# Layer 0's transfers taken off ScalarE: v written by GpSimd, blocks and rows loaded by SyncE

## The chip, the cores and the metric

The kernel runs on one core of one Trainium2 chip. A core has a matrix engine (TensorE, PE in the profile; its weight loads are shown as PEld), a vector engine (VectorE, DVE), an engine for activations and copies (ScalarE, ACT), a general engine (GpSimd, POOL) and a sequencer that only issues transfers and waits (SyncE, SP). Transfers can be issued by SyncE, ScalarE and GpSimd, each with a queue of its own (q1, q10 and q0 in the profile); all queues are served by the same 16 DMA engines. Each engine works through its own list of instructions in order and waits where an instruction needs something that another engine or a transfer has not delivered. The metric is the time of one execution on the device in microseconds (us).

## What is computed

An input x of 8 images of 56 x 56 pixels with 384 channels goes through two layers in float32, each of the form x + conv(groupnorm(x)). The "conv" of a layer is an attention over 3 x 3 neighbourhoods:

```python
# layer 0: 12 heads, a 9 x 9 attention per pixel and head
v = einsum('bhwc,oc->bhwo', x, Wv)
patches = the 3 x 3 neighbours of each pixel of v, zero outside the image
a = einsum('bhwc,oc->bhwo', x, Wa).reshape(b, n, heads, 9, 9)
attn = softmax(a * d ** -0.5, axis=-1)
out = einsum('bnhpq,bnqhd->bnphd', attn, patches)
# each of the 9 rows p of out is added back to the neighbour that it belongs to, then
y = einsum('bhwc,oc->bhwo', canvas, Wo)
# layer 1: 6 heads, one row of 9 weights per pixel and head, biases, no adding back
```

The group norm has 32 groups over whole images, so its statistics must be complete before a layer's values of that image are used.

## The kernel before

Images are taken two at a time: four pairs. Within a pair the work goes by image columns: 56 columns of 2 x 56 = 112 pixels, which lie on the partitions. Eight columns make a group, and since 7 tiles of 128 rows hold the 8 x 112 pixels, the eighth column's pixels ride along in the last 16 rows of the seven tiles; at the eighth step no tile is computed.

Layer 0 is one loop over 4 x 56 steps and three more. A step is `attend` for one column, with pieces of other work put between its matmuls by `between`:

- TensorE projects the column's normalised input `xn` on the attention weights `wa_t` in three parts into PSUM banks (three banks, used in turn). VectorE takes the maximum and subtracts it into `at`, ScalarE applies the exponential, then TensorE makes the values in another bank and ScalarE copies them to `v`, which has two buffers.
- `spread` writes v to a table in DRAM, `vtab0`, laid out by patches of 7 columns with 2 columns of margin on each side. A column that two patches need is written twice by one transfer. The last 16 rows are written to the place of the group's eighth column, by one or two further transfers. In the kernel before these two or three transfers are issued by ScalarE right behind the copy of v.
- One step later `weigh` runs `normalise` (VectorE sums to `den`, GpSimd multiplies `at` by it) and, for the column before, `presum` (GpSimd adds neighbouring columns into `pre`). `share_out` sends the 16 rows of `at` to their place by GpSimd transfers (`last`, `at<-at`, `at<-last`).
- Three steps later `fold` turns `pre` into rows of weights `wts`: GpSimd clears a buffer, ScalarE fills two rows, TensorE shifts (`pw`), VectorE adds the rest, and SyncE writes it to a second table, `ztab0`. There are four `wts` buffers.
- Once in seven steps `fetch_v` loads a patch's values (`vp`, two transfers of 1536 KB) and, a step later, `fetch` its weights (`z`, two of 2352 KB) on SyncE. From four steps after that, `contract` multiplies them on TensorE into two PSUM tiles `pc`, which ScalarE copies to `yT`; `project_out` multiplies by the output weights into `po`, VectorE adds the residual `xres` into `x1t`, and SyncE stores it. These pieces are queued in `jobs`, two a step.

The input is made ready beside this. The pair's transposed input lies in DRAM (`xTs`). `load` brings a block of four columns into `xin`, of which there is one buffer, at the step where `j == NCH - 1`, that is once in four steps, behind the last `normed` that reads the block before; `normed` makes `xn` of it two steps later on ScalarE. For the next pair `stats_load` brings four columns of rows into `xr` (two buffers), once in three steps; TensorE transposes them (`pt`), ScalarE copies them to `xt`, VectorE takes statistics and SyncE writes them to `xTs`. In the kernel before, `load` and `stats_load` are issued by ScalarE, from `upkeep`, at the end of a step.

Two things set the order. In layer 0's loop every engine keeps the order of the program: `tc.keep_in_program_order` and the class `InOrder` (lines 124 to 134) record it. Transfers report through counters: those of SyncE and ScalarE share one set of eight, used in turn, those of GpSimd have another eight. A transfer is not issued until the one that used its counter before has landed.

Layer 1 is a second loop after this one. It is not touched; its own `spread` is already issued by GpSimd.

Of the kernel before, what the change touches and what calls it, by code (L numbers as in the profile page):

```python
# [15 lines left out]
def two_outlook_layers(  # L16
# [34 lines left out]
    B, H, W, C = x.shape  # L51
# [7 lines left out]
    SB = 8  # L59
# [266 lines left out]
    def spread(queue, table, width, col, pad, row, v, rows_of=None):  # L326

        (px, sx), *more = patches_of(col, pad)
        n, rows = 1 + len(more), v.shape[0]
        line = width * C  # L330
        first = (px * (R + GAP) + GAP + row) * line + sx * C
        queue.dma_start(  # L332
            bass.AP(
                table.tensor, table.offset + first,
                [
                    *([line * step, count] for step, count in rows_of or ((1, rows),)),
                    *([[(R + GAP) * line - PX * C, n]] if n > 1 else []), [1, C],
                ],
            ),
            v.unsqueeze(1).to_broadcast([rows, n, C]) if n > 1 else v,  # L340
        )
# [79 lines left out]
    def layer0(late, pools):  # L421
# [11 lines left out]
        def stats_load(pair, blk, queue, xr):  # L433
            queue.dma_start(xr, xf[pair * R : (pair + 1) * R, blk * XB : (blk + 1) * XB, :])
            xrs[pair, blk] = xr

        def xr_tile(pair, blk):
            return io.tile([P, XB, C], F32, tag="xr", name=f"xr_{pair}_{blk}")[:R]
# [121 lines left out]
        def load(g):  # L560
            pair, blk = divmod(g, NBLK)
            xins[g] = io.tile([P, NCH, XB, R], F32, tag="xin", name=f"xin_{g}", bufs=1)
            scalar.dma_start(
                xins[g].rearrange("p i m r -> p i (m r)"),
                xTs[pair][:, :, blk * XB * R : (blk + 1) * XB * R],
            )
# [24 lines left out]
        def attend(pair, c, between):  # L591

            nm = f"0_{pair}_{c}"
            k, j = divmod(c, SB)
            if j == NTILE:
                for n in range(K + 1):
                    between(n)
                return
            lhs = xns[(pair * W // SB + k) % 2][:, :, j, :]
            at = work.tile([P, K, K2, PH], F32, tag="at", name=f"at_{nm}", bufs=4)  # L600
            mx = work.tile([P, K, PH], F32, tag="mx", name=f"mx_{nm}", bufs=1)
            for pi in range(K):
                pl = bank(P, BANK - NP0, BANK)
                project(pl[:, :NL], lhs, wa_t, pi * NL, NL)
                pl = pl.rearrange("r (q a) -> r q a", q=K2)
                vector.tensor_reduce(mx[:, pi, :], pl.rearrange("r q a -> r a q"), AX.X, ALU.max)
                vector.tensor_tensor(
                    at[:, pi], pl, mx[:, pi, :].unsqueeze(1).to_broadcast([P, K2, PH]), ALU.subtract
                )
                between(pi)  # L610
            scalar.activation(at, at, AF.Exp, scale=SCALE0)
            attns[pair, c] = at
            pv = bank(P, 0, C)
            project(pv, lhs, wv_t, 0, C)
            v = work.tile([P, C], F32, tag="v", name=f"v_{nm}")
            scalar.copy(v, pv)
            spread(scalar, vtab0, SX0, c, 2, 0, v[:R])
            end = c - j + NTILE
            if len([*patches_of(end, 2)]) == 1:
                spread(scalar, vtab0, SX0, end, 2, j * PART, v[R:], ((H, IMG), (1, PART)))  # L620
            else:
                for b in range(IMG):
                    lo = R + b * PART
                    spread(scalar, vtab0, SX0, end, 2, b * H + j * PART, v[lo : lo + PART])
            between(K)

        def share_out(pair, c):

            k, j = divmod(c, SB)
            at, last = attns[pair, c], lasts[(pair * W // SB + k) % 2]  # L630
            if j < NTILE - 2:
                gpsimd.dma_start(
                    bass.AP(
                        last.tensor, last.offset + j * PART * NA0,
                        [[H * NA0, IMG], [NA0, PART], [1, NA0]],
                    ),
                    at[R:].rearrange("p a b c -> p (a b c)"),
                )
                return
            end = c - j + NTILE  # L640
            if j == NTILE - 2:
                attns[pair, end] = work.tile([P, K, K2, PH], F32, tag="at", name=f"at_0_{pair}_{end}", bufs=4)
                for b in range(IMG):
                    n = b * H + j * PART
                    gpsimd.dma_start(
                        attns[pair, end][b * H : n].rearrange("p a b c -> p (a b c)"), last[b * H : n]
                    )
            for b in range(IMG):
                n, lo = b * H + j * PART, R + b * PART
                gpsimd.dma_start(attns[pair, end][n : n + PART], at[lo : lo + PART])  # L650
# [184 lines left out]
        def upkeep(step):  # L835

            pair, c = divmod(step, W)
            if pair == 0:

                for n in (2 * step, 2 * step + 1):  # L840
                    if n < NBLK:
                        keep_block(0, (0, 1, 4, 2, 3)[n] if n < 5 else n)
                if c == 1:
                    gpsimd.memset(wts, 0.0)
                if c == 3:
                    sync.dma_start(wo_t, wo0.rearrange("(i p) n -> p i n", p=P))
                if c == 8:
                    for z in zs:
                        nc.gpsimd.memset(z, 0.0)
            while clearing and clearing[0][0] <= step:  # L850
                clearing.pop(0)[1]()
            if pair + 1 < NPAIR:
                blk, i = divmod(c - 3, NCH)
                if 0 <= c and i == 0 and blk < NBLK - 1:
                    stats_load(pair + 1, blk + 1, scalar, xr_tile(pair + 1, blk + 1))
                if NBLK * NCH + 3 <= c < NBLK * NCH + 6:
                    if c == NBLK * NCH + 3:
                        making["0"] = norm_params(stats.pop(pair + 1), f"0_{pair + 1}", params, pair + 1)
                    next(making["0"])
            g, j = divmod(step + 2 * XB, XB)  # L860
            if j < NCH and g < NPAIR * NBLK:
                normed(g, (j,))
            if step < NCH:
                normed(1, (step,), shared=False)
            if j == NCH - 1 and 2 < g + 1 < NPAIR * NBLK and g > 2:
                load(g + 1)
# [14 lines left out]
        for step in range(NPAIR * W + LAG):  # L881
            folding = fold(*divmod(step - LAG, W)) if step >= LAG else iter(())
            turning = turned(step)

            def weigh():

                normal = 1 <= step < NPAIR * W + 1 and (step - 1) % SB < NTILE
                if normal:
                    normalise(*divmod(step - 1, W))
                if normal and step % SB == NTILE:  # L890
                    share_out(*divmod(step - 1, W))
                if 2 <= step < NPAIR * W + 2:
                    presum(*divmod(step - 2, W))
                if normal and step % SB < NTILE:
                    share_out(*divmod(step - 1, W))

            def between(n):

                if n == 0:
                    next(turning, None)  # L900
                    weigh()
                    jobs.run(step, 1)
                elif n == 1:
                    next(folding, None)
                    next(turning, None)
                elif n == 2:
                    jobs.run(step, 1)
                else:
                    next(folding, None)
                    if step % SB == NTILE:  # L910
                        jobs.run(step, 1)

            if step < NPAIR * W:
                attend(*divmod(step, W), between)
                upkeep(step)
            else:
                for n in range(K + 1):
                    between(n)
            flush()

            pair, c = divmod(step - LAG - PX, W)
            if pair >= 0 and c % PX == 0:
                fetch_v(pair, c // PX)
            pair, c = divmod(step - LAG - PX - 1, W)
            if pair >= 0 and c % PX == 0:
                fetch(pair, c // PX, step + 4)
# [336 lines left out]
```

## Time and profile before

| | us |
|---|---|
| three runs | 3550.32, 3551.01, 3561.62 |
| median | 3551.01 |
| profiled execution | 3572.52 |
| its span, from first to last instruction | 3570.8 |
| busy in the span: PE, DVE, POOL, ACT | 3252.5, 1861.3, 1409.7, 1303.7 |
| idle of PE between 71 and 2345 us (layer 0's loop) | 235.6 |
| mean granted PE clock in that stretch, share of full | 0.95 |

The profile is of one execution, whose own time is 21.5 us above the median. A row of instructions gives the line, the engine, the operation, what is written and what is read, how often, the busy time, the mean time of one in ns, and the idle time of the engine just before it with what ended it. Since all work goes through recording helpers, most instructions have line 119, 122 or 134, and are told apart by the names of what they write and read. A row of waits names who waited, for whom, the total, how often and the longest. [...] PE's granted clock is either 1.0 or 0.5 in the records of this run; a mean in between is a mixture over time.

### The profile page before, as it was taken

Reading aid. Unit: us, or ns where it says so; the run is one execution under the profiler, and the core shown is the slowest. Engines: PE = TensorE matmul, PEld = TensorE weight load, DVE = VectorE, ACT = ScalarE, POOL = GpSimd, SP = SyncE. Lnnn points to the kernel's source line nnn. Section 1 sums busy time; section 2 is a strip of 40 time slices with the busy share of each in tenths; the row PEclk is TensorE's granted clock in tenths of the full one; section 3 lists DMA queues with packets and bytes.
Section 4 is the critical chain, followed back from the end, with each engine's and each line's share of the span. In section 5 each row is a group of like instructions: output and inputs, shape, how many; then the busy total and the mean of one; then the engine's idle time right before and its main releaser. Section 6 shows DMA issues by size and latency. Waiting matters only on the chain.

```text
span 3570.8 us, 74251 instructions
## 1 busy us (share of the span) xinstructions
PE 3252.5 (91%) x28510; PEld 2222.9 (62%) x28510; DVE 1861.3 (52%) x4454; ACT 1303.7 (37%) x3315; POOL 1409.7 (39%) x2468
## 2 busy tenths in 40 slices
PE   7777889999898999998998999978999999999998
PEld 5555666666666666666765666645666666666665
DVE  5555665666676666666666577623223323333332
ACT  4333334333333333333433333322434343434432
POOL 2543454444455544455545555531212222222220
PEclk7889999999999999999999999988999999999998
DMA  6788897787788876888786678786787787878785
GB/s 194 227 279 257 271 292 247 247 278 261 247 258 270 268 241 224 272 280 278 223 261 229 218 258 270 234 282 181 215 218 222 220 224 217 230 217 230 213 226 146
DMA packets 618370, 859.13 MB, mean 241 GB/s; under 512 B 207255, under 2 KB 508503, under 8 KB 613919
## 3 DMA queue, kind: packets, MB, share of 16 engines
q1 hardware_dynamic: 445310, 600.76, 54.6%
q10 hardware_dynamic: 127968, 145.91, 13.8%
q0 software_dynamic: 44736, 107.72, 9.6%
q8 instruction: 224, 3.67, 0.4%
q14 instruction: 132, 1.07, 0.1%
HBM read 520.28 MB, written 330.40 MB: 238 GB/s over the span
## 4 chain that ended last, share of the span: by engine, by line
PE 61%; DMA 21%; DVE 7%; issue 4%; ACT 3%; POOL 2%; ACTq 1%; SPq 1%; DVEq 0%; POOLq 0%
PE bank L119 32%; PE po L119 15%; PE pc L119 8%; DMA z<-ztab 6%; DMA ztab<-wts 4%; DMA at<-lgtab 3%; DMA lgtab<-lgt 3%; PE pw L119 2%; ACT xn L134 2%; DMA x<-x1t 2%; DVE den L134 1%; DVE d L134 1%; PE pt L122 1%; DMA xr<-in_x 1%; DVE mx L134 1%
## 5 line engine op out<-in xcount | busy, mean ns | idle before, releaser
L119 PE MATMUL bank<-wa_t,xn 128*128 128x288 f32 x3528 | 984.1, 417 | 35.4 <-ACT xn L134 27.0
L119 PE MATMUL po<-yT,wo_t 128*128 128x448 f32 (+1 forms) x2304 | 831.6, 501 | 47.5 <-DVE x1t L134 44.9
L119 PEld LDWEIGHTS bank<-wa_t,xn 128*128 128x128 f32 x3528 | 660.9, 195 | 253.2 <-issue 26.4
L134 POOL TENSOR_TENSOR at<-at,den 128x972 f32<-128x972 f32 x196 | 441.2, 2251 | 935.2 <-DVE den L134 613.7
L119 PEld LDWEIGHTS po<-yT,wo_t 128*128 128x128 f32 x2304 | 430.8, 192 | 339.6 <-issue 190.1
L332 POOL DMA_DIRECT2D vtab<-v x392 | 214.0, 549 | 846.1 <-DVE v L134 822.4
L119 PE MATMUL pc<-z,vp 121*32 121x49 f32 (+1 forms) x17664 | 390.0, 225 | 138.4 <-ACT yT L134 116.1
L134 DVE TENSOR_REDUCE mx<-bank 128x36 f32<-128x324 f32 x588 | 285.5, 486 | 438.2 <-PE bank L119 435.3
L134 ACT ACTIVATE at<-at 128x972 f32<-128x972 f32 (+1 forms) x228 | 215.4, 945 | 767.9 <-DVE at L134 767.8
L119 PE MATMUL bank<-wc_t,xn 128*128 128x438 f32 x1176 | 482.5, 547 | 2.2 <-ACT xn L134 2.2
L119 PEld LDWEIGHTS pc<-z,vp 121*32 121x32 f32 (+1 forms) x17664 | 352.2, 126 | 205.9 <-ACT yT L134 131.0
L119 PE MATMUL bank<-wv_t,xn 128*128 128x384 f32 x1176 | 436.8, 509 | 1.4 <-issue 1.4
L685 POOL TENSOR_TENSOR pre<-at,at 112x108 f32<-112x108 f32 (+1 forms) x440 | 244.1, 555 | 220.7 <-DMA at<-at 78.1
L119 PEld LDWEIGHTS bank<-wc_t,xn 128*128 128x128 f32 x1176 | 215.9, 193 | 173.7 <-issue 166.9
L134 ACT ACTIVATE xn<-xin,bias,scale 128x168 f32<-128x168 f32 (+1 forms) x474 | 208.4, 502 | 315.1 <-DMA vtab<-v 173.4
L119 PEld LDWEIGHTS bank<-wv_t,xn 128*128 128x128 f32 x1176 | 228.4, 198 | 144.0 <-issue 26.3
L134 DVE TENSOR_TENSOR at<-bank,mx 128x324 f32<-128x324 f32 x588 | 291.4, 496 | 44.1 <-POOL pre L683 13.8
L134 ACT COPY yT<-pc 128x294 f32<-128x294 f32 (+2 forms) x512 | 196.4, 406 | 232.3 <-PE pc L119 227.6
L134 DVE SCALAR_TENSOR_TENSOR x1t<-po,bo_t,x1t 128x448 f32<-128x448 f32 (+1 forms) x156 | 97.6, 626 | 248.5 <-PE po L119 248.5
L134 DVE TENSOR_TENSOR lgt<-bank,ba_t 128x54 f32<-128x54 f32 x196 | 41.6, 212 | 350.5 <-PE bank L119 350.5
L134 ACT ACTIVATE wts<-pre,inside 112x48 f32<-112x48 f32 (+4 forms) x672 | 180.1, 358 | 79.7 <-POOL pre L683 29.0
L134 ACT COPY ot<-pt 112x384 f32<-112x384 f32 x128 | 61.5, 481 | 380.0 <-PE pt L122 325.0
(112 smaller groups left out, 3123.1 us busy)
## 6 DMA issues: line engine op xcount, KB each, us to landing
z<-ztab SPq DMA_DIRECT2D x64, 2352.0 KB
vp<-vtab SPq DMA_DIRECT2D x64, 1536.0 KB
vp<-vtab SPq DMA_DIRECT2D x64, 945.0 KB
xres<-xT SPq DMA_DIRECT2D x32, 1176.0 KB
ztab<-wts SPq DMA_DIRECT2D x336, 110.2 KB
xin<-xT ACTq DMA_DIRECT2D x52, 672.0 KB
vtab<-v ACTq DMA_DIRECT2D x100, 336.0 KB
z<-ztab SPq DMA_DIRECT2D x128, 258.4 KB
```

Of the source, the lines that this page charges most:

```text
L119: tc.keep_in_program_order(nc.tensor.matmul(*args, **kwargs))
L122: tc.keep_in_program_order(nc.tensor.transpose(*args, **kwargs))
L134: return lambda *args, **kwargs: tc.keep_in_program_order(op(*args, **kwargs))
L332: queue.dma_start(bass.AP(table.tensor, table.offset + first, [*([line * step, count] for step, count in rows_of or ((1, rows),)), *([[(R ...
L685: nc.gpsimd.tensor_tensor(dst, terms[0], terms[1], ALU.add)
```

## The change

In layer 0's loop ScalarE issues no transfer any more. The writes of v move from the end of `attend` to a new function `keep_v`, which the following step calls at the end of `weigh`; GpSimd issues them, behind `normalise`, `presum` and `share_out` of that step. The loads of `xin` and `xr` stay where they are in the program, and SyncE issues them. Sizes, targets and buffers are the same.

```diff
         def load(g):
             pair, blk = divmod(g, NBLK)
             xins[g] = io.tile([P, NCH, XB, R], F32, tag="xin", name=f"xin_{g}", bufs=1)
-            scalar.dma_start(
+            sync.dma_start(
                 xins[g].rearrange("p i m r -> p i (m r)"),
...
             v = work.tile([P, C], F32, tag="v", name=f"v_{nm}")
             scalar.copy(v, pv)
-            spread(scalar, vtab0, SX0, c, 2, 0, v[:R])
+            vs[pair, c] = v
+            between(K)
+
+        def keep_v(pair, c):
+
+            j, v = c % SB, vs.pop((pair, c))
+            spread(gpsimd, vtab0, SX0, c, 2, 0, v[:R])
             end = c - j + NTILE
             if len([*patches_of(end, 2)]) == 1:
-                spread(scalar, vtab0, SX0, end, 2, j * PART, v[R:], ((H, IMG), (1, PART)))
+                spread(gpsimd, vtab0, SX0, end, 2, j * PART, v[R:], ((H, IMG), (1, PART)))
             else:
                 for b in range(IMG):
                     lo = R + b * PART
-                    spread(scalar, vtab0, SX0, end, 2, b * H + j * PART, v[lo : lo + PART])
-            between(K)
+                    spread(gpsimd, vtab0, SX0, end, 2, b * H + j * PART, v[lo : lo + PART])
...
-                    stats_load(pair + 1, blk + 1, scalar, xr_tile(pair + 1, blk + 1))
+                    stats_load(pair + 1, blk + 1, sync, xr_tile(pair + 1, blk + 1))
...
                 if normal and step % SB < NTILE:
                     share_out(*divmod(step - 1, W))
+                if normal:
+                    keep_v(*divmod(step - 1, W))
```

More of the change, by code (lines that the diff above doesn't have):

```diff
@@ L623, in attend @@
                     lo = R + b * PART
-                    spread(scalar, vtab0, SX0, end, 2, b * H + j * PART, v[lo : lo + PART])
-            between(K)
+                    spread(gpsimd, vtab0, SX0, end, 2, b * H + j * PART, v[lo : lo + PART])
+        vs = {}
         def share_out(pair, c):
```

## The prediction

> **What bounds the kernel now.** I read first the busy time in stretches, for layer 0's loop (71 to 2345 us) and for one of its holes:
>
> ```profile
> core 0: us, PE busy (x) PEld busy (x) DVE busy (x) ACT busy (x) POOL busy (x), PEclk, DMA share, GB/s
> 71.00:2345.00 2274.00, 2038.36 (x19092) 1453.87 (x19094) 1458.57 (x3555) 821.71 (x1942) 1136.33 (x1947) 0.95 0.79 255
> ...
> 964.50:979.50 15.00, 7.07 (x136) 5.53 (x125) 6.10 (x14) 4.85 (x14) 6.68 (x12) 0.77 0.78 244
> ```
>
> TensorE is busy 2038.4 of the loop's 2274 us: it is the bound, and 235.6 us of idle time are all that removed waits can give, apart from the clock. Next the waits of PE and ACT in the same stretch (total us, times, longest):
>
> ```profile
> PE pc L119 <- ACT yT L134: 93.2, 20, 10.8
> PE po L119 <- DVE x1t L134: 40.1, 24, 12.3
> PE pt L122 <- ACT xt L134: 29.8, 9, 10.9
> PE pw L119 <- POOL pre L683: 23.6, 10, 7.2
> PE bank L119 <- ACT xn L134: 20.9, 7, 5.5
> ```
>
> ```profile
> ACT xn L134 <- DMA vtab<-v: 173.4, 79, 12.4
> ...
> ACT xn L134 <- DMA ztab<-wts: 42.9, 13, 9.5
> ```
>
> PE waits mostly for copies by ScalarE, and ScalarE waits ahead of xn, the work that stands behind v's writes in its program. The timeline shows one case, first ScalarE, then TensorE:
>
> ```profile
> 963.91 0.46 ACT L134 COPY v<-bank 128x384 f32<-128x384 f32 x1
> 971.79 2.08 ACTq L134 DMA_DIRECT2D vtab<-v  x2
> 973.91 1.59 ACT L134 ACTIVATE xn<-xin,bias,scale 128x168 f32<-128x168 f32 x4 [9.54 <-DMA ztab<-wts]
> 975.41 0.51 ACT L134 COPY xt<-pt 128x448 f32<-128x448 f32 x1
> 975.83 0.70 ACT L134 COPY yT<-pc 128x294 f32<-128x294 f32 x2
> ```
>
> ```profile
> 966.72 1.63 PE L119 MATMUL bank<-wa_t,xn 128*128 128x288 f32 x6
> 976.28 2.19 PE L119 MATMUL pc<-z,vp 121*32 121x49 f32 x96 [7.93 <-ACT yT L134]
> ```
>
> ScalarE has finished v at 964.4 but issues its write only at 971.8. The row names what ended the wait: a write of ztab that SyncE had issued. SyncE's and ScalarE's transfers take turns on eight completion counters, so an issue waits until the transfer that had its counter before has landed. That one stood behind the two loads of z issued at 946.1, and v's write, xn, xt and yT stood behind it. PE lost 7.93 us.
>
> **The change, part by part.**
>
> *ScalarE's issues go.* 476 writes of v, 52 loads of xin and 42 of xr leave ScalarE; its stretches between an ACT instruction's end and the last issue add up to 470 us. Most of it costs nothing, as ScalarE is busy 822 of 2274 us. What counts is PE's idle time. I went through PE's gaps over 0.5 us in this stretch one by one: 27 began while, or within 4 us after, ScalarE had stood over 2.5 us at an issue of v. Crediting each with the smaller of the gap and of the standing above 0.55 us an issue gives 110.7 us (10.9, 10.8, 9.4, 7.9 are the largest). This is the first term: **-111**.
>
> *The clock.* In the hole above the granted clock is 0.77, in the loop 0.95. PE was busy for 170 us of the half-rate pieces, which cost 85 us against full rate. The holes credited are 111 of 235.6 us idle, 47%; so I credit 47% of 85: **-40**.
>
> *xin and xr go to SyncE's queue.* 94 issues at 0.57 us (xin's median on ScalarE) are 53 us on SyncE, which in this stretch waits 541 us for wts alone; they cost nothing as such. The load of xin now waits on SyncE for xn of the same step, and behind it stand the next ztab writes, which wait for VectorE's sums anyway, or in some steps a fetch of vp or z, with 5 us of margin at the matmuls (z of the case above had landed at 957.9, its first use is at 963.4). What counts is landing. On ScalarE's queue xin issued at 951.7 landed at 961.0, while z on SyncE's queue landed at 968.7. Behind z it lands after 968.7 plus 2.7 us of its own. I took for each xin the landing of what SyncE had issued before it, plus 2.7 us, and held it against its first use, less the hole that I remove: seven loads are late by 0.4 to 2.3 us (12.4 us) and four by 1.6 to 5.9 us (17.4 us). All of these 30 us on PE's path, with clock in the same ratio (40/111), cost **+41**; nothing if ScalarE's slack hides them. xr, reckoned the same way, has at least 2.8 us left in each case: 0; past that PE's transposes would stand for it directly.
>
> *v's writes go to GpSimd, a step later.* The prices of issues there:
>
> ```profile
> L332 POOL DMA_DIRECT2D vtab<-v x392 | 214.0, 549 | 846.1 <-DVE v L134 822.4 <-issue 11.7 <-DMA z<-ztab 11.5
> ...
> L134 POOL DMA_DIRECT2D last<-at x140 | 86.5, 618 | 1.2 <-POOL at L134 1.2
> ```
>
> 476 issues at 0.549 us (the same write in layer 1) are 261 us; by the row of last, 294. GpSimd idles 2274 - 1136 = 1138 us, so in most steps they fall into its wait for den (935 us ahead of the products at). They are 1.1 to 1.65 us a step, ahead of the memset of wts, which ScalarE reads some 5 us later (1204.5 and 1209.4). In 19 of 196 steps the wait for den is under 1.5 us; these are the seventh columns of the groups of eight, where the chain goes on over a transfer to PE:
>
> ```profile
> 1226.89 1.01 POOL L134 DMA_DIRECT2D at<-at  x2
> 1227.89 0.33 POOL L134 MEMSET wts<- 112x120 f32 x1
> 1229.64 2.25 POOL L134 TENSOR_TENSOR at<-at,den 128x972 f32<-128x972 f32 x1 [1.42 <-DVE den L134]
> ...
> 1238.66 0.41 POOL L685 TENSOR_TENSOR pre<-at,at 112x108 f32<-112x108 f32 x1 [3.06 <-DMA at<-at]
> ```
>
> The later writes hide in the 3.06 us before 1238.66; the earlier ones delay the product by up to 1.65 us. PE waited for pre 10 times. Low bound 0, if the delays end in PE's queue of other work; high bound 28 groups x 1.65 = 46, and 24 more if at's copies wait behind v's bytes for 3 us in the 8 groups that meet a load of z. I take 10 x 1.5: **+15**, nearest to the ten rows seen.
>
> *The buffer of v.* There are two, so the copy of column c+2 waits until v of c has been read. In the short steps, copies two apart are 15.3 us apart; GpSimd gets to the place of the issue 7.8 to 8.2 us after the copy, plus 1.1, so 6.0 us are left for a write that I put at the 5.2 us median and 8.3 us longest of last's transfers on that queue. A lateness of 2.3 us is less than the 4 us until PE needs that bank again. I take **+5**; the high bound is 60 short steps x 2.3 = 138, and 0 the low one. [...]
>
> *What is late next.* In the hole VectorE itself stood 2.41 us for a ztab write (7 such waits, 15.6 us in the loop); these stay: **+15**, between 0 and the 40 of PE's waits for x1t.
>
> Sum: -111 - 40 + 41 + 15 + 5 + 15 = **-75 us**. Against the profiled execution's 3572.5 (span 3570.8) that is 3497; it stands 21.5 us above the median of the runs shown, 3551.0, so the prediction is **3476**.
>
> **Rivals.**
> 1. *The holes go whole.* Nothing new waits: -151, 3400. For it: xin's lateness is small against GpSimd's and ScalarE's idle time. Against: DMA engines are already 0.92 busy at 940 to 964.5.
> 2. *The loads take the wait over.* One queue drains in order, so each xin, xr and ztab write behind 4.7 MB of z is as late as ScalarE was. If half of the 32 patches, not 11 loads, cost 5.3 us and a third of that in clock, the loss is 16 x 7 = 112 on top of the other 35: 3547, no change. For it: ztab issued at 954.9 to 957.8 landed only at 971.4, v's write issued at 956.9 on the other queue at 964.3. [...]
> 3. *Slower: the copy of v waits for GpSimd's write.* If the writes land not 5 to 7 but over 10 us after issue, behind each other and behind z, then margin and bank cover (6 + 4 us) are both gone, and the 60 short steps bind at GpSimd's pace: at 13 us, 60 x 3 = 180 against the 75 gained: 3656; it decides against the change from an 11.3 us landing on. Against: longest row 8.3 us; for: 168 to 336 KB a write, where last has 60.8.
>
> **How the numbers follow.** A measurement of this kernel tells about 0.3% (11 us) from no change. Chances: forecast (3430 to 3525) 0.50, whole gain 0.15, loads take over (3525 to 3575) 0.15, slower by GpSimd's write (3575 and up) 0.20. Faster is the first two and a third of the third: 0.70; same 0.08; slower 0.22. The range runs from 3405, just above the whole gain, to 3585, a third of the way into the slow case: it leaves out 0.07 and 0.13.
>
> **What would show it.** Right: no wait of ACT xn for vtab; PE's wait of pc for yT under 40 us; the loop's PEclk above 0.96; some 261 us more on POOL. xin's step: ACT xn waits for DMA xin 30 us. Wrong: ACT v waiting for vtab's writes by over 100 us, PE pw for pre well over 40, or PE's idle time as before under other names, xin or xr.

## The result, and the profile after

The changed kernel takes 3529.23 us (median of seven runs, 3520.71 to 3542.84); the kernel before, run beside it, 3557.60 (seven runs, 3550.32 to 3573.44). The ratio is 0.9923, 95% interval 0.9899 to 0.9947: 0.8% shorter, 28 us, where 75 were forecast; the whole interval lies below 1. The profiled execution after is one of 3529.23 us, at its median, while the one before (3572.52) lies 15 us above its median; so the two traces differ by 43 us, of which 28 stand in the medians. What is read from the two traces below holds some 15 us that belong to that one execution.

The page of the changed kernel, first the engines' busy time, then v's writes in the groups of instructions (line, engine, operation, count; busy us, mean ns; idle before):

```profile
PE 3245.5 (92%) x28510; PEld 2213.4 (63%) x28510; DVE 1865.4 (53%) x4454; ACT 1297.7 (37%) x3315; POOL 1680.1 (48%) x2944
...
L134 POOL DMA_DIRECT2D vtab<-v x476 | 285.8, 605 | 16.2 <-DMA vtab<-zeros 7.0
```

The stretch of layer 0's loop, in the columns that the prediction shows for before:

```profile
71.00:2302.50 2231.50, 2034.70 (x19097) 1445.08 (x19099) 1461.66 (x3554) 814.01 (x1942) 1406.75 (x2423) 0.95 0.80 259
```

The loop is 42.5 us shorter: 38.8 of it is PE's idle time (235.6 to 196.8), 3.7 its busy time. The granted clock is 0.95 as before. Layer 1 is where it was (1225.8 and 1225.0 us). What PE waits for in the loop of the changed kernel (us in total, times, longest):

```profile
PE po L119 <- DVE x1t L134: 64.2, 29, 8.4
PE pt L122 <- DMA xr<-in_x: 52.3, 7, 14.5
PE pw L119 <- POOL pre L690: 41.7, 13, 7.2
PE pc L119 <- ACT yT L134: 8.0, 8, 2.9
...
PE bank L119 <- ACT xn L134: 4.3, 6, 1.0
```

The waits for ScalarE are nearly gone: yT, xt and xn were 93.2 + 29.8 + 20.9 = 143.9 us and are 8.0 + 0 + 4.3 = 12.3. In their place stands a wait that the kernel before did not have, 52.3 us for rows `xr`, and those for x1t and pre have grown by 24.1 and 18.1. 131.6 us went and 94.5 came.

ScalarE and VectorE in the same stretch:

```profile
ACT xn L134 <- DMA xin<-xT: 30.0, 8, 12.2
...
ACT v L134 <- DMA vtab<-v: 17.6, 17, 2.5
```

```profile
DVE x1t L134 <- DMA xres<-xT: 59.6, 8, 11.8
```

xn waits 30 us for its block, and PE hardly notices (4.3 us for xn). The copy of v waits for GpSimd's write 17 times, at most 2.5 us. Ahead of x1t, VectorE waits 59.6 us in eight places for the residual `xres`.

The largest new hole, first SyncE's queue (its issues stand as SPq) and then PE, in the timeline of the changed kernel (start, us, instruction, and in brackets the idle time before it with what ended it):

```profile
197.72 1.29 SPq L134 DMA_DIRECT2D z<-ztab  x2
199.11 6.37 SPq L134 DMA_DIRECT2D ztab<-wts  x2
205.53 1.36 SPq L134 DMA_DIRECT2D xr<-in_x  x1
```

```profile
204.53 2.10 PE L119 MATMUL bank<-wv_t,xn 128*128 128x384 f32 x6
221.13 0.98 PE L122 MATMUL pt<-ident,xr 112*128 112x112 f32 x4 [14.50 <-DMA xr<-in_x]
222.04 2.19 PE L119 MATMUL pc<-z,vp 121*32 121x49 f32 x96
```

SyncE issues xr at 205.5 to 206.9, behind the two loads of z (4.7 MB) and two writes of ztab. It lands at 221.0, 14 us after its issue; PE has been ready for its transposes since 206.6 (204.53 + 2.10), and the contractions pc stand behind them in PE's order.

Four of the seven waits for xr are of this kind, behind the loads of z: 14.5, 3.6, 4.8 and 3.8 us, 26.7 in sum. The other three, 8.0, 9.8 and 7.7 us, 25.6 in sum, have no load of z ahead. There SyncE clears parts of the tables and issues xr behind that, as in the last of them:

```profile
303.57 6.47 SPq L215 DMA_DIRECT2D ztab<-zeros  x6
310.13 1.56 SPq L134 DMA_DIRECT2D xr<-in_x  x1
```

```profile
322.02 1.01 PE L122 MATMUL pt<-ident,xr 112*128 112x112 f32 x4 [7.72 <-DMA xr<-in_x]
```

### The profile page after: what moved, and what is told of

Read it like the earlier page. It is cut to its first block, busy times and chain, and to the rows that moved or that the text cites. A ratio compares the mean times of both kernels' runs of the same rounds, so it can differ in the third digit from the quotient of the medians.

```text
span 3527.5 us, 74596 instructions
## 1 busy us (share of the span) xinstructions
PE 3245.5 (92%) x28510; PEld 2213.4 (63%) x28510; DVE 1865.4 (53%) x4454; ACT 1297.7 (37%) x3315; POOL 1680.1 (48%) x2944
## 4 chain that ended last, share of the span: by engine, by line
PE 67%; DMA 16%; DVE 6%; issue 4%; POOL 3%; ACT 2%; SPq 1%; DVEq 0%; POOLq 0%; ACTq 0%
PE bank L119 37%; PE po L119 17%; PE pc L119 8%; DMA lgtab<-lgt 3%; PE pw L119 3%; DMA xr<-in_x 3%; DMA at<-lgtab 2%; DMA xres<-xT 2%; PE pt L122 2%; DMA ztab<-wts 1%; POOL at L134 1%; DVE den L134 1%; ACT xn L134 1%; DVE d L134 1%; DMA z<-ztab 1%
## 5 line engine op out<-in xcount | busy, mean ns | idle before, releaser
L332 POOL DMA_DIRECT2D vtab<-v x392 | 213.9, 549 | 840.0 <-DVE v L134 807.6
L119 PE MATMUL bank<-wv_t,xn 128*128 128x384 f32 x1176 | 425.8, 499 | 0.6 <-issue 0.6
L692 POOL TENSOR_TENSOR pre<-at,at 112x108 f32<-112x108 f32 (+1 forms) x440 | 236.2, 538 | 137.6 <-DVE wts L134 81.6
L134 POOL DMA_DIRECT2D vtab<-v x476 | 285.8, 605 | 16.2 <-DMA vtab<-zeros 7.0
L134 ACT ACTIVATE wts<-pre,inside 112x48 f32<-112x48 f32 (+4 forms) x672 | 182.3, 361 | 89.7 <-POOL pre L690 58.3
```

The lines of the kernel that those rows point to most:

```text
L119: tc.keep_in_program_order(nc.tensor.matmul(*args, **kwargs))
L134: return lambda *args, **kwargs: tc.keep_in_program_order(op(*args, **kwargs))
L332: queue.dma_start(bass.AP(table.tensor, table.offset + first, [*([line * step, count] for step, count in rows_of or ((1, rows),)), *([[(R ...
L692: nc.gpsimd.tensor_tensor(dst, terms[0], terms[1], ALU.add)
```

## The experiments

Every kernel ran beside the kernel before, on the same chip; each computes everything. "Loop" is layer 0's loop in the profiled execution, from 71 us to 16.7 us past the last copy of v.

| run | v's writes | xin, xr | further | median us (before) | ratio, 95% interval | loop us | PE idle in it |
|---|---|---|---|---|---|---|---|
| before | ScalarE | ScalarE | | 3557.6 | | 2274.0 | 235.6 |
| after | GpSimd | SyncE | | 3529.2 (3557.6) | 0.9923, 0.9899 to 0.9947 | 2231.5 | 196.8 |
| e11_after_again | GpSimd | SyncE | the same kernel | 3520.4 (3547.0) | 0.9926, 0.9904 to 0.9948 | 2221.5 | 202.9 |
| e3_v_only | GpSimd | ScalarE | | 3514.0 (3562.9) | 0.9875, 0.9851 to 0.9899 | 2209.0 | 182.3 |
| e4_loads_only | ScalarE | SyncE | | 3522.3 (3562.9) | 0.9889, 0.9870 to 0.9908 | 2224.2 | 210.7 |
| e9_loads_gpsimd | ScalarE | GpSimd | | 3514.7 (3547.0) | 0.9911, 0.9884 to 0.9938 | 2243.2 | 207.5 |
| e1_xr_early | GpSimd | SyncE | xr a step earlier | 3519.0 (3562.9) | 0.9878, 0.9851 to 0.9904 | 2214.6 | 191.9 |
| e2_xr_gpsimd | GpSimd | SyncE, GpSimd | | 3515.8 (3562.9) | 0.9878, 0.9857 to 0.9899 | 2217.4 | 188.1 |
| e5_xres_early | GpSimd | SyncE | xres a step earlier | 3499.3 (3571.5) | 0.9811, 0.9781 to 0.9841 | 2203.6 | 183.1 |
| e6_keep_late | GpSimd, late | SyncE | | 3530.9 (3571.5) | 0.9890, 0.9870 to 0.9910 | 2217.9 | 202.8 |
| e7_all_early | GpSimd, late | SyncE | xr, xres earlier | 3478.0 (3571.5) | 0.9746, 0.9722 to 0.9769 | 2167.5 | 158.7 |
| e10_post5 | GpSimd, late, one put off | SyncE | xr, xres earlier | 3459.5 (3547.0) | 0.9755, 0.9731 to 0.9779 | 2160.4 | 153.2 |
| e8_v_only_xres | GpSimd | ScalarE | xres earlier | 3511.4 (3571.5) | 0.9840, 0.9816 to 0.9864 | 2202.5 | 173.6 |
| e12_same_step | GpSimd, same step | SyncE | | 3506.7 (3547.0) | 0.9884, 0.9861 to 0.9906 | 2223.9 | 204.6 |

The medians of the kernel before differ between the four sets of runs (3547 to 3571), so it is ratios that are compared across sets.

### What the new waits cost: xr

The load of xr is moved one step ahead of its place, or given to GpSimd's queue where it does not stand behind z.

```diff
-                blk, i = divmod(c - 3, NCH)
-                if 0 <= c and i == 0 and blk < NBLK - 1:
+                blk, i = divmod(c - 2, NCH)
+                if c == 0:
+                    stats_load(pair + 1, 0, sync, xr_tile(pair + 1, 0))
+                elif 2 <= c and i == 0 and blk < NBLK - 1:
```

```diff
-                    stats_load(pair + 1, blk + 1, sync, xr_tile(pair + 1, blk + 1))
+                    stats_load(pair + 1, blk + 1, gpsimd, xr_tile(pair + 1, blk + 1))
```

> The changed kernel, with each load of xr issued one step earlier, still by SyncE. Theory 1 (the gain was lost because xr, now in SyncE's queue behind the loads of z, reaches PE's transposes late: 52.3 us in the changed kernel's profile): a step is 8 to 10 us, five of the seven waits are shorter than that, so PE pt <- DMA xr falls to 15 us or less and the time to about 3529 - 45 = 3485, ratio to the kernel before 0.980. Theory 2 (it was lost on GpSimd, whose issues of v delay wts and pre, and SyncE behind them): PE takes the wait up again under po or pw, the time stays within 10 us of 3529.

> The changed kernel, with the loads of xr issued by GpSimd, at the same place in the program. Theory 1 (queue order behind z): the loads land 5 to 10 us after issue whatever z does, PE pt <- DMA xr falls under 10 us, the time to about 3485. Theory 2 (GpSimd is the loss): 42 more issues at about 0.6 us, 25 us more on GpSimd; PE pw <- POOL pre grows from 41.7 and the time is 3529 or more.

PE's waits in the loop of the kernel with the early xr, and of that with xr on GpSimd's queue:

```profile
PE po L119 <- DVE x1t L134: 80.3, 30, 14.1
...
PE pc L119 <- ACT yT L134: 21.1, 12, 7.2
...
PE pt L122 <- DMA xr<-in_x: 7.2, 1, 7.2
```

```profile
PE po L119 <- DVE x1t L134: 77.9, 30, 19.5
...
PE pc L119 <- ACT yT L134: 19.2, 11, 6.9
```

The waits for xr go from 52.3 to 7.2 and to none: the cause is where the load stands in SyncE's queue and when it is issued, as both cures work. But the wait for x1t grows by 16 and 14 us and that for yT by 13 and 11, so that the ratio falls by 0.0045 only (16 us), where 45 were expected, and its interval still meets the changed kernel's. PE had its next stop a few us further on. The 7.2 us that are left with the early xr stand behind six clearing writes, not behind z.

### What comes next: xres

The next stop is the residual. VectorE adds `xres` into x1t; the load of xres is issued behind a patch's first contraction, and in the changed kernel it comes, in 13 of 31 cases, right behind a load of xin or xr on SyncE, in the kernel before in none. That cannot be all: the wait for x1t is as long where xin and xr are on another queue (60.1 and 59.7 us in two kernels below). The row of x1t begins within 0.2 us of the landing of xres in 7 of 31 patches before and in 13 after. Here the load is issued a step ahead of the first contraction:

```diff
+            xloads.append((due - 1, load_x))
...
-                        later.append(
-                            lambda: sync.dma_start(
-                                fetched["x"], xTs[pair][:, :, px * T : (px + 1) * T]
-                            )
-                        )
...
+                while xloads and xloads[0][0] <= step:
+                    xloads.pop(0)[1]()
```

> The changed kernel, with each load of xres issued one step ahead of the first contraction instead of behind it. Theory 1a (the holes moved: once ScalarE no longer stands, PE reaches project_out before xres has landed): PE po <- DVE x1t falls from 64 to about 25 us (the short waits for PSUM remain), the time by 30 to 45 us, to 3485 to 3500. Theory 3 (behind every wait that is removed the next one stands, because the loop is held by something common, such as the transfers' bandwidth in the bursts): po falls, but the sum of PE's idle time stays at 190 us or more, and the time falls by less than 15 us.

PE's waits in the loop of this kernel:

```profile
PE pt L122 <- DMA xr<-in_x: 59.0, 7, 14.9
...
PE po L119 <- DVE x1t L134: 25.8, 23, 4.3
```

The wait for x1t falls from 64.2 to 25.8, that for xr stays, and the ratio is 0.9811: 0.0112 below the changed kernel, some 40 us, with intervals apart, as theory 1a expected. The order of this load is untouched by the change.

### GpSimd's order, and everything together

v's writes stand ahead of the clearing of wts on GpSimd, and SyncE, waiting for wts, stands longer (318.7 us before, 521.0 after). In the next kernel they are issued behind it, in `between(2)`.

```diff
-                if normal:
-                    keep_v(*divmod(step - 1, W))
...
+                    if 1 <= step < NPAIR * W + 1 and (step - 1) % SB < NTILE:
+                        keep_v(*divmod(step - 1, W))
```

> The changed kernel, with v's writes issued by GpSimd later in the same step, behind fold's clearing of wts instead of ahead of it. Theory 2 (v's issues ahead of the clearing hold back wts, the ztab writes and SyncE): SyncE's wait for POOL wts falls from 521 to about 320 us, PE pw <- POOL pre from 41.7 towards 24, the time by 20 to 30 us to about 3500. Theory 1: the order on GpSimd matters for pw alone, 10 us or less: 3520 to 3530.

What SyncE waits for in the loop of the changed kernel, and of this one:

```profile
SPq L134 <- POOL wts L134: 521.0, 132, 10.4
SPq L134 <- DVE wts L134: 481.2, 108, 41.9
```

```profile
SPq L134 <- DVE wts L134: 560.7, 123, 44.5
SPq L134 <- POOL wts L134: 394.5, 140, 8.4
```

SyncE stands 126.5 us less for GpSimd's clearing, but 79.5 us longer for VectorE's sums, and PE's wait for pre is 40.0 after 41.7. The wait for the clearing does not reach the 320 us of theory 2, and its 20 to 30 us of gain do not show. By itself this cannot be told from the changed kernel: the intervals of the ratio overlap (0.987 to 0.991, 0.990 to 0.995).

All three edits, xr early, xres early and v's writes late, go into one kernel.

> The changed kernel with all three: xr a step earlier, xres a step earlier, v's writes behind the clearing of wts. Theory 1: the terms add: xr 45, xres 35, pw 15 and some 20 for the clock are 115 us, 3529 - 115 = 3415 to 3440. Theory 3: 3490 or more, with PE's idle time in layer 0's loop still 170 us or more under other names.

What PE waits for in its loop:

```profile
PE pw L119 <- POOL pre L690: 46.2, 14, 8.3
PE po L119 <- DVE x1t L134: 39.3, 24, 12.5
...
PE pt L122 <- DMA xr<-in_x: 4.7, 1, 4.7
```

The ratio is 0.9746, the lowest of all: 93.5 us under the kernel before. Its loop is 64.0 us shorter than the changed kernel's. The three edits alone had shortened it by 16.9, 27.9 and 13.6 us, 58.4 in sum; by the ratios, which rest on more than one execution, they gave 0.0045, 0.0112 and 0.0033 alone and 0.0177 together. So they add, but to some 63 us and not to the 115 of theory 1; the time lies between the two theories. What the change gave by itself was 28 us; more than that lay behind the two late loads. Whether the early xres would help the kernel before as much was not tried. What is left on top is the wait for pre, 46.2 us.

In the step behind the sixth column of each group the writes of v stand between the transfers of at and pre; there they are put off by a step.

```diff
-                        keep_v(*divmod(step - 1, W))
+                        if (step - 1) % SB == NTILE - 1:
+                            keep_v(*divmod(step - 2, W))
+                        if (step - 1) % SB != NTILE - 2:
+                            keep_v(*divmod(step - 1, W))
```

> All three loads and the writes of v as in the kernel of everything early (3478 us), but in the step behind the sixth column of a group the writes of v are put off by one step, so that they no longer stand on GpSimd between share_out's chain and pre. Theory 1 (TensorE's waits for pre come from v's issues standing ahead of pre on GpSimd in that step): the wait for pre falls from 46 us to about 25, as with v on ScalarE, and the time by 15 to 20 us, to about 3460, ratio 0.970 to the kernel before. Theory 2 (the waits for pre are spread over all steps, by v's issues in general): the wait for pre stays above 40 us and the time within 8 us of 3478.

The same view of this kernel:

```profile
PE po L119 <- DVE x1t L134: 42.2, 24, 14.7
PE pw L119 <- POOL pre L690: 41.9, 13, 7.2
```

The wait for pre stays above 40 us and the ratio is the same within its interval (0.9755). That is what theory 2 expected, but its picture of waits in all steps does not hold. Counted by the column that is folded, 26.7 of the 41.9 us fall on the sixth of a group's eight, as do 31.4 of 46.2 in the kernel of everything early, 34.9 of 41.7 in the changed kernel and 15.2 of 23.6 in the kernel before. That is the place at which this edit aimed, so v's issues in that step hold little of it; what holds pre there stays open.

### Each half alone

Writes of v alone, then loads alone:

```diff
-            sync.dma_start(
+            scalar.dma_start(
...
-                    stats_load(pair + 1, blk + 1, sync, xr_tile(pair + 1, blk + 1))
+                    stats_load(pair + 1, blk + 1, scalar, xr_tile(pair + 1, blk + 1))
```

> One part alone: v's writes by GpSimd a step later, xin and xr loaded by ScalarE as before. Theory 1: xr and xin have their own queue again, PE pt <- DMA xr is gone; but ScalarE can again stand for a completion counter, at 94 issues instead of 570. If those stands are as rare as their count, a sixth of 470 us, the holes of copies by ScalarE are under 30 us and the time is 3480 to 3500. Theory 2: as the changed kernel, 3529, or slower.

> The other part alone: xin and xr loaded by SyncE, v written by ScalarE in its own step. Theory 1: ScalarE stands at v's writes as before (143.9 us of PE's waits for its copies), and xr comes late on top, though partly inside the same holes: 3557 to 3610. Theory 2: the loads cost nothing, so the time is that of the kernel before, 3557 within 10.

PE's waits in the loop where v alone has moved, and where the loads alone have:

```profile
PE po L119 <- DVE x1t L134: 60.1, 29, 13.4
PE pw L119 <- POOL pre L690: 48.6, 14, 8.2
PE pc L119 <- ACT yT L134: 24.5, 9, 11.4
```

```profile
PE po L119 <- DVE x1t L134: 56.6, 27, 8.0
PE pt L122 <- DMA xr<-in_x: 49.2, 6, 16.9
PE pw L119 <- POOL pre L683: 24.3, 11, 7.2
PE pc L119 <- ACT yT L134: 21.3, 14, 4.4
PE bank L119 <- ACT xn L134: 18.3, 7, 5.8
```

Three things follow. Each half gives at least as much as both together, so their gains do not add: both take away the same holes. No theory expected it: v alone came out between its two forecasts, and the loads alone were to bring nothing or a loss. The wait for xr comes with the loads (49.2 here, none with v alone), and the added wait for pre with v's writes (48.6 against 24.3). And with the loads alone the holes go although ScalarE still issues v: its stretches up to v's issues fall from 424 us (of the 470 at all its issues) to 289, those of over 6 us from 17 to 2. Moving v was not needed for that.

Two explanations offered themselves: with fewer transfers in turn the counters that SyncE and ScalarE share come free sooner; or z lands sooner when no load of another queue runs beside it, and so lets its counters go. The trace of the kernel before records these counters: its 1908 transfers of SyncE and ScalarE report on the same eight, 238 or 239 on each, GpSimd's 764 on eight others. Between two issues on one of the shared eight at most 16 reports came, the number of one transfer, and 216 of the 1900 issues on a counter used before began within 0.3 us of the last report of the transfer that had it. With the loads alone the first cannot be it, since SyncE and ScalarE issue the same 1908 transfers between them as before. In the next kernel v stays on ScalarE, and the two loads go to GpSimd: off the counters, but on a queue beside z.

```diff
-            scalar.dma_start(
+            gpsimd.dma_start(
...
-                    stats_load(pair + 1, blk + 1, scalar, xr_tile(pair + 1, blk + 1))
+                    stats_load(pair + 1, blk + 1, gpsimd, xr_tile(pair + 1, blk + 1))
```

> v's writes stay with ScalarE as in the kernel before; the loads of xin and xr are issued by GpSimd, so that they ride on a queue of their own beside z, as they did on ScalarE's, but take no counter of the eight that SyncE and ScalarE share. Theory 1 (it is the counters: with two kinds of transfer fewer in turn, ScalarE finds its counter free at v's issue more often): TensorE's waits for yT, xt and xn together fall from 144 us before to under 50, as in the kernel with SyncE's loads and v on ScalarE; about 3520 to 3530 us. Theory 2 (it is the loads beside z on another queue that make z land late and so hold the counters): those waits stay over 100 us, and the time is that of the kernel before less about 10 us at most, 3550 to 3560 by a kernel before of 3560.

PE's waits in the loop of this kernel:

```profile
PE po L119 <- DVE x1t L134: 59.7, 28, 12.1
PE pc L119 <- ACT yT L134: 52.2, 19, 9.7
PE pw L119 <- POOL pre L683: 26.3, 10, 7.2
PE pt L122 <- ACT xt L134: 26.1, 4, 10.3
PE bank L119 <- ACT xn L134: 17.0, 7, 4.5
```

Neither comes out clean. PE's waits for ScalarE are 52.2 + 26.1 + 17.0 = 95.3 us, near theory 2's bound and half way between before (143.9) and the loads on SyncE (39.6 for yT and xn, 51.8 with a single wait that is put down to at); ScalarE's stands of over 6 us are 9, between 17 and 2. The ratio, 0.9911, is theory 1's time. The p90 of z's landing (nine in ten have landed by then, counted from the end of the issue) is 20.1 us with the loads on GpSimd's queue, 21.0 on ScalarE's, 18.2 on SyncE's. So z still lands late here, and the holes shrink all the same, with 94 transfers fewer in turn. This fits both causes acting, which is not shown: the trace is of one execution, the slowest of its six, and the runs do not part the causes further.

The kernel with v alone was also run with xres early:

> v's writes by GpSimd a step later, xin and xr by ScalarE as before, xres loaded a step earlier. Theory 1: 3514 less 35 for PE po <- DVE x1t, 3480. Theory 3: within 15 us of 3514.

The wait of PE for x1t falls from 60.1 to 44.2 and the ratio from 0.9875 to 0.9840, which their intervals do not part: theory 3. With xin and xr on SyncE's queue the early xres took away more of the wait (64.2 to 25.8), though with xr early too 39.3 us of it are left.

### A repetition, and the step later

> The changed kernel again, beside the others of this call. All theories: ratio to the kernel before 0.989 to 0.995, as at first (0.9923); TensorE waits some 52 us for xr, 64 for x1t, 42 for pre.

The ratio is that of the first runs within 0.0003, and PE's waits within 2.3 us (x1t 65.7, xr 54.6, pre 40.3). Between the two profiled executions of this kernel it is the clock that differs most: PE was busy at half rate for 148.0 us of the loop in the first and 114.8 in the second, and busy for 2034.7 and 2018.6 us in all.

In the last kernel GpSimd writes v in v's own step:

```diff
             vs[pair, c] = v
+            keep_v(pair, c)
             between(K)
...
-                if normal:
-                    keep_v(*divmod(step - 1, W))
```

> The changed kernel, but GpSimd issues the writes of v in the step in which v is made, at the end of attend, and not a step later. Theory 1 (what matters is that ScalarE does not issue; GpSimd has time): within 10 us of the changed kernel. Theory 2 (the step later is needed: GpSimd, in order, would stand for ScalarE's copy of v, which comes last in attend, and so bring at and pre late): TensorE's wait for pre and VectorE's or GpSimd's waits grow, 20 us or more slower than the changed kernel.

GpSimd's waits in the loop of this kernel, and of the changed one:

```profile
POOL at L134 <- DVE den L134: 402.4, 169, 11.9
POOL vtab L134 <- ACT v L134: 223.3, 104, 46.0
```

```profile
POOL at L134 <- DVE den L134: 665.0, 166, 50.9
```

GpSimd now stands 223 us for ScalarE's copy, and 263 us less for den: for the most part it is the same waiting in another place. PE's wait for pre is 46.1 us after 40.3. The median is 14 us under the changed kernel's on the same chip, more than theory 1 allowed and opposite to theory 2; but the loops of the two profiles are 2223.9 and 2221.5 us, and what differs there is layer 1, which both leave alone (1214.6 and 1226.8 us, 11 of the 12 in PE's busy time). So the step later is not needed; whether writing at once is better stays open.

## Why the prediction was wrong in size

Term by term, in us of the loop, against what the two traces show:

| term | forecast | measured | read from |
|---|---|---|---|
| holes behind v's issues | -111 | -131.6 | PE's waits for yT, xt, xn: 143.9 to 12.3 |
| clock | -40 | -3.7 | PE busy 2038.4 to 2034.7 |
| xin | +41 | about 0 | ACT waits 30.0 for xin, PE's wait for xn is down to 4.3 |
| xr | 0 | +52.3 | PE's wait for xr, seven times |
| GpSimd's issues | +15 | +18.1 | PE's wait for pre: 23.6 to 41.7 |
| buffer of v | +5 | about 0 | ACT waits 17.6 for v's writes, PE for v 1.8 |
| what is late next | +15 | +24.1 | PE's wait for x1t: 40.1 to 64.2 |
| all else | | -1.7 | rest of PE's idle time |
| sum | -75 | -42.5 | loop 2274.0 to 2231.5 |

The direction was right, and so was the mechanism that carries it: the holes of PE behind ScalarE's stands at the issues of v were the gain, and they went, more wholly than credited. Of the points that were to show it, ACT's wait of xn for vtab is gone, PE's wait for yT is 8.0, under 40, POOL is 270.4 us busier (1406.75 - 1136.33; forecast 261; v's issues alone are 285.8, at 605 ns and not 549). The loop's clock did not rise above 0.96: it is 0.95, and 0.96 in the repetition. Of the signs of being wrong, PE's wait for pre is at 41.7, just over 40, and the wait for xr came. The first term took the cause too narrowly: it put the holes down to v's issues on ScalarE, yet with the loads alone moved most of them go while ScalarE still issues v.

**The step that failed is xr, "at least 2.8 us left in each case: 0".** A term put at nothing measured 52.3 us. It is the reverse of the xin step beside it: I forecast 30 us of xn's waiting for xin, and 30.0 came. (The 2.7 us that it counts for xin itself are an estimate: 672 KB at the 255 GB/s of the loop.) That the sums agree is luck, as eleven loads were to be late by 0.4 to 5.9 us and eight waits of 0.9 to 12.2 us came; but ScalarE's idle time hid them, as the sentence "nothing if ScalarE's slack hides them" allowed. The 2.8 us of xr are not in the trace of before. There xr is used 12.5 us after its issue in the tight cases (issued 195.4, used 207.9; 441.1, 453.5; 1022.8, 1035.3), and the loads of z that SyncE had issued ahead of it landed until 213.3, 458.9 and 1040.4: 5 us late each. Of all 42 loads, fourteen are used 0.2 to 6.7 us before everything ahead on SyncE has landed. The four worst of them, by 5.6 to 6.7 us, are the four that wait behind z in the changed kernel, 26.7 us. The other 25.6 us stand behind SyncE's clearing of the tables, which the working does not mention. PE itself waits for xr, in order, and no other engine's idle time lies between. The prediction had said so ("past that PE's transposes would stand for it directly"); only the slack was misread. The runs with xr early or on GpSimd's queue take the wait away. They gave back 16 of the 47 us by which the medians fell short, so this is the largest term that was mis-sized and not the whole. The clock, 36 us short, and the next late load stand beside it; the 41 us of xin that did not come, and holes worth 21 more, hid much of all that in the sum.

**What is late next** was put at 15, of bounds 0 to 40, and came to 24; but its weight is larger than that, since it takes back what a cure of xr gives (x1t 64.2 to 80.3). Only the two kernels with xr and xres early (and v's writes late) pass what was forecast: 93.5 and 87.5 us under the kernel before.

**GpSimd's issues** were put at 15 and came to 18.1. The size and the place, the end of a group, were right; that the issues ahead of the product cause it was not borne out, as the kernel that moves them away from there keeps most of the wait.

**The clock** was credited as if half-rate time followed the holes in proportion. It did not: 170.5 us of PE's busy time were at half rate before, 148.0 after, and in the repetition 114.8 with more idle time (202.9 us after 196.8). So the two executions of one kernel differ by 33 us. The clock records of the traces of before and after show stretches at 1.0 and at 0.5 in turn, each but the last a multiple of 3.41 us long (93 stretches before and 85 after; 6.83 and 10.24 us are the first two of the kernel before); what sets them off no run shows. Holes removed should have carried a clock term with bounds from 0, and the holes added one too.

**The rivals.** Rival 2, the loads take the wait over, holds for xr in seven places, four of them behind z, and not for 16 patches; the ratio measured, 0.9923, lies between the forecast's (3476 / 3551 = 0.979) and this rival's (3547 / 3551 = 0.999), nearer to the rival's. The order within a queue, on which it rests, is what the hole at 206.6 us shows: z landed at 208.4 and 217.9, xr, issued behind it, at 221.0. In the trace of the kernel before 1262 of SyncE's 1270 transfers have a landing that can be read, and all of them landed in the order of issue; after, two of 1354 landed ahead of the one issued before them, by 0.25 us at most. Rival 3 did not come: v's writes landed 5.7 us after issue in the median and 10.6 at most, under the 11.3 from which it decides. Rival 1 was right of the old holes and wrong on new ones.

## What to carry to other kernels

A transfer that moves to another engine's queue takes that queue's backlog (xr behind z on SyncE's queue, issued by 206.9, landed at 221.0): for each one, take its earliest use by an engine that is the bound, and the landing of all that stands ahead of it, and check the slack in the trace case by case. Lateness in front of an engine with idle time costs little (30 us of xin cost nothing that shows), in front of the bound it becomes the bound's idle time in full (52 us of xr). When holes are removed, expect the next late transfer behind them, and issue it a step earlier in the same change: here that was worth more (xr and xres) than the change.

## What the runs showed of the hardware

Which queue a load rides on went with how late the slowest of the others landed. With xin and xr on ScalarE's or GpSimd's queue, z on SyncE's had a p90 from issue to landing of 20.1 to 21.0 us in four kernels; with both on SyncE's queue 17.3 to 18.5 in nine; with xr alone on GpSimd's, 19.1. The medians hardly part: 14.0 to 15.6 us in the four, 13.3 to 14.8 in the nine. The bytes are the same. The choice also moved the order of landing: behind z on SyncE's queue xr landed up to 14.1 us after its issue, on GpSimd's queue 9.7 at most.

Layer 1, which no kernel touches, took 1212.9 to 1236.8 us in the fourteen profiles, and PE's time at half rate in one kernel differed by 33 us between two executions. A gain smaller than that spread, some 24 us, in one trace of this kernel is not to be read as an effect without repeated runs.
